# A fused attention and feed-forward layer on one core: W_o by seven quarters, sums with one PSUM operand, two roots at a time, another tail

## The chip, the cores and the metric

One NeuronCore of one Trainium2 chip runs the whole kernel. The metric is the device time of one execution in microseconds. The engines are TensorE (PE, matmuls; PEld is its weight load), VectorE (DVE), ScalarE (ACT) and GpSimd (POOL); SyncE (SP) issues most DMAs. [...] Matmuls write PSUM[...]; the rest of the working data is in SBUF.

## What is computed

Cut to what matters, with x of shape (4, 2048, 256) and everything in fp32:

```python
# attention within chunks of C = 32 tokens, decayed and causal
Q, K, V = x @ W_q.T, x @ W_k.T, x @ W_v.T
S = (Qc @ Kc.T) * mask                  # mask[i, j] = decay ** (i - j), 0 for j > i
O = S @ Vc
a = x + (sigmoid(x @ W_g.T) * O) @ W_o.T + x
h = layernorm(a)                        # over the 256 features, eps 1e-5, no scale or bias
# feed-forward with int32 weights in -127..127, scaled by 1/127
r = h + (silu(h @ w_gate.T) * (h @ w_up.T)) @ w_down.T   # 256 -> 768 -> 256
out = layernorm(r)
```

## The kernel before, in words

**Blocks.** The 8192 tokens are 16 blocks (NB) of 512 (TB), each of four groups (NG) of 128. D = 256 is two chunks of 128 features and H = 768 six. x comes in twice, token by row (`x`) and feature by row (`xT`). For Q and K the kernel has one matrix M = Wq^T Wk, so that scores are x M x^T. `attn_gate`, `attn_v` and `attn_y` are plain projections and are used for blocks 0 and 1 alone.

**Seven quarters.** From block 2 on, V, y = x M and the gate are made by `seven` (L390): a product of two 2x2 arrangements of quarters with seven products of quarters in place of eight. `token_sums` (L348, POOL) and `weight_sums` (L335) make the sums of quarters that go in. The first four products go to four PSUM banks; the other three are added later onto banks 1, 5 and 7 (`others`, the "rest" in the loop). Between them ACT copies p1, p5 and p7 to SBUF (L406), DVE makes u = p6 + p1 (L408) and POOL p57 = p5 + p7 (L410). At the end ACT evicts the first quarter (L416), DVE the second and third (L417, L418, with u), and POOL makes the fourth from p57 and u (L419). `token_major` (L374) writes tokens by row with matmuls of 128x128, `feature_major` (L359) features by row with 128x256.

**Attention.** `attn_scores` (L506) takes pairs of chunks, 64 tokens, into bank ps and masks them with DVE (L524) into sT. `attn_values` (L529) makes po = v^T sT, which DVE multiplies by the gate (L542) into goT. `attn_out` (L576) multiplies goT by W_o through `project_back` (L551; matmul L561, bank pa, 128x256), adds 2x (L582), and calls `layer_norm` (L310): DVE statistics (L295, L296), ACT square root (L304), DVE reciprocal and scaling (L315, L317), and four DVE operations (L319), one for each group. Square root and sigmoid are in different tables of ACT, so a table load stands before each change (the rows of L304, L441 and L664 that say ACT_TABLE_LOAD). h is held times 2^23 (H_UP).

**Feed-forward.** h is transposed: in the loop by `move_h` (L609), four DVE transposes in squares of 32 and 16 DMAs on SP, and `split_h` (L630), which cuts it into a high part (ACT, fp32r) and a low one (POOL, fp16). In six chunks `ffn_up` (L646) makes fg and fu (L656, one bank each), a sigmoid (ACT, L664), s = fg * s (DVE, L666), u = fu * s (DVE, L668), and u's high part (ACT, L675) and low part (POOL, L676). `ffn_down` (L678) calls `project_back` (fdn), DVE adds h (L683), and `finish` (L695) normalizes and stores.

**Order.** One loop (L734 to L779) runs b from 0 to 13: the feed-forward of block b, scores, values and out-projection of block n = b + 2, projections of block m = b + 3. They are interleaved by hand as written there. Each engine keeps its own queue; the order within a queue is made by the framework from the program and its dependences, save where an instruction is pinned with `keep_in_program_order` (`in_turn`). PSUM banks go round by eight under one tag (ps), so a tile waits for whoever last read its bank. Blocks 14 and 15 end the program by hand (from L787): the feed-forward of 14 with the transposition of h_15 by PE (L598), block 15's `ffn_up` in two halves of 256 columns, and its fdn one group at a time (L853, residual L861), with moments, root and `normalize` (L803: DVE reciprocal L806, POOL shift L815, ACT scaling L824) for each; the last group is normalized by DVE (L876, L877).

**Wide weights.** `look_up` (L258) takes the largest magnitude of the six halves of the weights (L261, one at each of the first six turns of the loop); `count_wide` (L270) compares them, sums over partitions with a small matmul (pw, L277), and gives n_wide, called just before block 15's fdn. A branch for weights beyond 127 uses n_wide after the end; these inputs don't take it.

Of the kernel before, what the change touches and what calls it, by code (L numbers as in the profile page):

```python
# [54 lines left out]
P = 128  # L55
# [10 lines left out]
U_UP = 2.0**-3  # L66
WARM = 2
# [3 lines left out]
def kernel(  # L71
# [184 lines left out]
    top = const.tile([P, 6], F32, tag="top", name="top")  # L256

    def look_up(i):  # L258
        w = (fg, fu, fd)[i // 2][0].bitcast(F32)
        half = w.shape[1] // 2  # L260
        reduced = nc.vector.tensor_reduce(  # L261
            top[:, i : i + 1],
            w[:, i % 2 * half : (i % 2 + 1) * half, :].rearrange("p k n -> p (k n)"),
            mybir.AxisListType.X,
            ALU.max,
            apply_absolute_value=True,
        )
        tc.keep_in_program_order(reduced)
# [21 lines left out]
    def moments(r, name, groups=range(NG), order=free):  # L290

        mv = small.tile([P, NG, 2], F32, tag="mv", name=f"mv_{name}")
        for g in groups:
            st = small.tile([P, 6], F32, tag="st", name=f"st_{name}_{g}")
            order(nc.vector.bn_stats(st, r[:, g, :]))  # L295
            order(nc.vector.bn_aggr(mv[:, g, :], st))  # L296
        return mv
# [12 lines left out]
    def layer_norm(dst, r, name, on_r=1.0, on_dst=1.0):  # L310


        mv = moments(r, name)
        rstd = root(mv, name, on_r)
        nc.vector.reciprocal(rstd, rstd)  # L315
        if on_dst != on_r:
            nc.vector.tensor_scalar(rstd, rstd, on_dst / on_r, None, ALU.mult)  # L317
        for g in range(NG):
            nc.vector.tensor_scalar(  # L319
                dst[:, g, :],  # L320
                r[:, g, :],
                mv[:, g, 0:1],
                rstd[:, g : g + 1],
                ALU.subtract,
                ALU.mult,
            )
# [21 lines left out]
    def token_sums(t, name):  # L348

        out = sums.tile([P, 4, HB], F32, tag="sums", name=f"{name}_sums")  # L350
        t1, t3, t2, t4 = (out[:, i, :] for i in range(4))
        b11, b12, b21, b22 = (t[:, k, n * HB : (n + 1) * HB] for k in range(2) for n in range(2))
        nc.gpsimd.tensor_tensor(t1, b12, b11, ALU.subtract)
# [5 lines left out]
    def feature_major(a, b):  # L359


        def product(i, pb, first):
            nc.tensor.matmul(  # L363
                pb,
                lhsT=a[i - 1],
                rhs=b[i - 1],
                start=first,
                stop=True,
                skip_group_check=True,
            )  # L370

        return product

    def token_major(a, b):  # L374


        def product(i, pb, first):
            for g in range(HB // P):
                nc.tensor.matmul(  # L379
                    pb[:, g * P : (g + 1) * P],  # L380
                    lhsT=b[i - 1][:, g * P : (g + 1) * P],
                    rhs=a[i - 1],
                    start=first and g == 0,
                    stop=True,
                    skip_group_check=True,
# [4 lines left out]
    def seven(name, product, quarter, func=AF.Copy):  # L390
# [9 lines left out]
        banks = {i: bank(f"p{i}_{name}")[:, :HB] for i in (1, 5, 7, 6)}  # L400
        p = {}
        for i, pb in banks.items():
            product(i, pb, True)
            if i != 6:
                p[i] = part(f"p{i}")
                nc.scalar.copy(p[i], pb)  # L406
        u = part("p6")
        nc.vector.tensor_tensor(u, banks[6], p[1], ALU.add)  # L408
        p57 = part("p57")
        nc.gpsimd.tensor_tensor(p57, p[5], p[7], ALU.add)  # L410

        def others():
            for i, onto in ((2, 1), (3, 5), (4, 7)):
                product(i, banks[onto], False)
            c11, c12, c21, c22 = (quarter(i, j) for i in range(2) for j in range(2))
            nc.scalar.activation(c11, shaped(banks[1], c11), func)  # L416
            nc.vector.tensor_tensor(c12, shaped(banks[5], c12), shaped(u, c12), ALU.add)  # L417
            nc.vector.tensor_tensor(c21, shaped(banks[7], c21), shaped(u, c21), ALU.add)  # L418
            nc.gpsimd.tensor_tensor(c22, shaped(p57, c22), shaped(u, c22), ALU.add)  # L419
# [86 lines left out]
    def attn_scores(b, yT):  # L506
# [16 lines left out]
        for rows in halves:  # L523
            nc.vector.tensor_tensor(  # L524
                sT[rows, :, rows], ps[rows], mask[rows], ALU.mult
# [3 lines left out]
    def attn_values(b, sT, v, sg):  # L529
        goT = work.tile([P, KD, TB], F32, tag="goT", name=f"goT_{b}")  # L530
        for dc in range(KD):
# [10 lines left out]
            nc.vector.tensor_tensor(goT[:, dc, :], po, sg[:, dc, :], ALU.mult)  # L542
# [33 lines left out]
    def attn_out(b, goT, up=H_UP):  # L576
# [3 lines left out]
        def residual(gs, pb):  # L580

            nc.vector.scalar_tensor_tensor(  # L582
                flat(r, gs), flat(xn, gs), 2.0, pb, ALU.mult, ALU.add
            )

        project_back(b, (chunked(goT),), (chunked(wo),), residual, "pa")
        layer_norm(r, r, f"a{b}", on_dst=up)
        return r

# [19 lines left out]
    def move_h(b, h):  # L609
# [5 lines left out]
        for g in range(NG):  # L615
            nc.vector.transpose(
                sq[:, :, g, :], h[:, g, :].rearrange("p (j f) -> p j f", f=SQ)
# [28 lines left out]
    def ffn_up(b, hT, uT, chunks, cols=slice(0, TB)):  # L646
        n = cols.stop - cols.start
        for hc in chunks:
# [16 lines left out]

            nc.vector.scalar_tensor_tensor(s, pg, U_UP / H_UP**2, s, ALU.mult, ALU.mult)  # L666
            u = work.tile([P, n], F32, tag="u", name=f"u_{b}_{hc}")
            nc.vector.tensor_tensor(u, pu, s, ALU.mult)  # L668
# [5 lines left out]
            hi, lo = uT[0][hc][:, cols], uT[1][hc][:, cols]  # L674
            nc.scalar.copy(hi, u)  # L675
            nc.gpsimd.tensor_tensor(lo, u, hi.bitcast(F32), ALU.subtract)  # L676

    def ffn_down(b, uT, h):  # L678
        r = work.tile([P, NG, D], F32, tag="r2", name=f"r2_{b}")

        def residual(gs, pb):
# [3 lines left out]
            )  # L685

        project_back(b, uT, [chunked(w) for w in fd], residual, "fdn")
        return r
# [6 lines left out]
    def finish(b, r, start=None):  # L695
        layer_norm(r, r, f"f{b}", on_r=H_UP)
# [8 lines left out]
    yT = attn_y(0)  # L705
    v_1 = attn_v(1)
    fg = integers(ffn_gT, ffn_int[0], "fg")
# [9 lines left out]
    sT_1 = attn_scores(1, yT)  # L717
    xTs[3] = load_xT(3)
# [13 lines left out]
    looked = 0  # L732

    for b in range(NB - 2):  # L734
# [6 lines left out]
        yT, v, sg = ahead  # L741
        ffn_up(b, hT, uT, range(0, 1))
# [7 lines left out]
        moving = move_h(b + 1, hs[b + 1])  # L750
# [3 lines left out]
        ffn_up(b, hT, uT, range(3, 4))  # L754
        if more:
            v_rest()
        goT = attn_values(n, sT, v, sg)
        if more:
            y_next, y_rest = split_y(m, x_sums)
        ffn_up(b, hT, uT, range(4, 5))  # L760
        if more:
            y_rest()
            hTs[b + 1] = split_h(b + 1, moving)
        ffn_up(b, hT, uT, range(5, KH))
        if more:
            sg_next, g_rest = split_gate(m, x_sums)
        hs[n] = attn_out(n, goT, 1 if n == NB - 1 else H_UP)
        if more:
            g_rest()
            ahead = y_next, v_next, sg_next  # L770
        if m + 1 < NB:
            x_sums = token_sums(xTs[m + 1], f"x_{m + 1}")
        r = ffn_down(b, uT, hs.pop(b))
        if not more:
            hTs[b + 1] = split_h(b + 1, moving)
        finish(b, r)
        if looked < top.shape[1]:
            look_up(looked)
            looked += 1  # L779
    for i in range(looked, top.shape[1]):  # L780
        look_up(i)
# [15 lines left out]
    r_before = ffn_down(last - 1, uT, hs[last - 1])  # L797
    mv_before = moments(r_before, f"f{last - 1}")
    ffn_up(last, hTs[last], uT_last, range(len(early), KH), cols[0])
    ffn_up(last, hTs[last], uT_last, range(KH), cols[1])  # L800
    n_wide = count_wide()

    def normalize(r, mv, rstd, name, on_r=1.0, groups=range(NG)):  # L803

        span = slice(groups[0], groups[-1] + 1)
        in_turn(nc.vector.reciprocal(rstd[:, span], rstd[:, span]))  # L806
        if on_r != 1:
            in_turn(
                nc.vector.tensor_scalar(
                    rstd[:, span], rstd[:, span], 1 / on_r, None, ALU.mult  # L810
                )
            )
        shift = small.tile([P, NG], F32, tag="shift", name=f"shift_{name}")
        for g in groups:
            nc.gpsimd.tensor_scalar(  # L815
                shift[:, g : g + 1],
                mv[:, g, 0:1],
                rstd[:, g : g + 1],
                -1.0,
                ALU.mult,  # L820
                ALU.mult,
            )
        for g in groups:
            scaled = nc.scalar.activation(  # L824
                r[:, g, :],
                r[:, g, :],
                AF.Identity,
                bias=shift[:, g : g + 1],
                scale=rstd[:, g : g + 1],
            )  # L830
            in_turn(scaled)

    std_before = root(mv_before, f"f{last - 1}", H_UP, order=in_turn)
    r = work.tile([P, NG, D], F32, tag="r2", name=f"r2_{last}")

    def store_group(g):
        tokens = slice(last * TB + g * P, last * TB + (g + 1) * P)
        nc.sync.dma_start(out[tokens, :], r[:, g, :])

    waiting = []

    def normalize_first():
        g, mv, std = waiting.pop(0)
        normalize(r, mv, std, f"f{last}_{g}", groups=[g])
        store_group(g)

    for g in range(NG):
# [16 lines left out]
        if g == 0:  # L866
            normalize(r_before, mv_before, std_before, f"f{last - 1}", H_UP)
            store(last - 1, r_before)
        std = root(mv, f"f{last}_{g}", groups=[g], order=in_turn)
        waiting.append((g, mv, std))  # L870
        if 0 < g < NG - 1:
            normalize_first()
        if g == NG - 2:
            normalize_first()
# [119 lines left out]
```

## Time and profile before

| | |
|---|---|
| median of three runs | 536.26 us (535.37 to 536.46) |
| the profiled execution | 535.63 us |
| its span in the profile | 533.9 us |
| what lies around the span | 1.7 us |
| one block of the loop | 32.0 us |
| PE's last matmul ends | 524.3 us into the span |
| DVE's last normalization ends | 529.0 us |

Views of the profile used here: the page (busy time of each engine, and shares of the chain of work that ended last); the waits of an engine (who it waited for, us in total, times, longest); windows (busy time of each engine in a stretch); the chain in order of time; the timeline of an engine (start and length in us, engine, line, operation, out<-in with partitions x elements, in square brackets the idle time before it and who ended it); and groups of instructions by form (busy us, mean ns of one, idle before). L numbers are lines of the kernel of that profile. A "record" is one matmul in the trace; an fp32 matmul leaves two.

### The profile page before, as it was taken

The numbers are of one execution on the slowest core, as the hardware profiler recorded it, in microseconds if no ns is written. First come the engines' busy times: TensorE is split into PE (matmuls) and PEld (weight loads), VectorE is DVE, ScalarE is ACT, GpSimd is POOL, SyncE is SP. The second block draws the span as 40 slices with busy tenths as digits, with TensorE's granted clock in tenths as the row PEclk, the third lists the DMA queues.
The fourth block names the chain that finished last, engine by engine and source line by source line (L and its number), as shares of the span: only waits on it lengthen the run. The fifth ranks groups of instructions, "written<-read, shape, count | busy, mean of one in ns | idle before, by whom it ended". The sixth has DMA issues, their size and how long they took to land.

```text
span 533.9 us, 9939 instructions
## 1 busy us (share of the span) xinstructions
PE 522.8 (98%) x3486; PEld 421.0 (79%) x3486; DVE 391.2 (73%) x1026; ACT 310.8 (58%) x561; POOL 268.4 (50%) x305
## 2 busy tenths in 40 slices
PE   8999999999999999999999999999999999999992
PEld 5688887888878788887888878788887888868792
DVE  4468659587695867859587695867859587698883
ACT  2284556555564754656555664764657566566754
POOL 5132672735636365572735636374572736433651
PEclk9999999999999999999999999999999999999997
DMA  7531312214130231412214130231412113020102
GB/s 253 181 120 39 80 40 69 52 41 119 42 101 18 52 108 41 114 46 63 58 39 120 41 105 15 54 107 40 112 49 78 42 43 78 1 65 16 40 2 82
DMA packets 43126, 36.87 MB, mean 69 GB/s; under 512 B 4673, under 2 KB 38977, under 8 KB 43073
## 3 DMA queue, kind: packets, MB, share of 16 engines
q1 hardware_dynamic: 41952, 35.15, 23.3%
q10 hardware_dynamic: 1088, 1.05, 0.6%
q8 instruction: 29, 0.48, 0.4%
q14 instruction: 25, 0.20, 0.1%
q0 software_dynamic: 32, 0.00, 0.0%
HBM read 20.45 MB, written 8.39 MB: 54 GB/s over the span
## 4 chain that ended last, share of the span: by engine, by line
PE 95%; DVE 2%; ACT 1%; issue 0%; DVEq 0%; POOL 0%
PE fg L656 16%; PE fdn L561 16%; PE fu L656 15%; PE pa L561 10%; PE p_v L379 8%; PE p_y L363 8%; PE p_g L363 8%; PE po L535 5%; PE ps L514 3%; PE pg L459 1%; PE py L475 1%; PE pv L494 1%; PE pi L177 1%; DVE u L668 1%; DVE s L666 1%
## 5 line engine op out<-in xcount | busy, mean ns | idle before, releaser
L676 POOL TENSOR_TENSOR u_lo<-u,u_hi 128x512 f16<-128x512 f32 (+1 forms) x102 | 123.7, 1214 | 144.3 <-ACT u_hi L675 143.8
L666 DVE SCALAR_TENSOR_TENSOR s<-fg,s 128x512 f32<-128x512 f32 (+1 forms) x102 | 66.4, 651 | 48.1 <-ACT s L664 47.6
L664 ACT ACTIVATE s<-fg 128x512 f32<-128x512 f32 (+1 forms) x102 | 58.2, 571 | 66.6 <-PE fg L656 65.9
L675 ACT CAST u_hi<-u 128x512 fp32r<-128x512 f32 (+1 forms) x102 | 60.4, 592 | 31.5 <-DVE u L668 30.7
L656 PE MATMUL fg<-hT_hi,fg_hi 128*128 128x512 f32 (+1 forms) x204 | 74.0, 443 | 0.0
L668 DVE TENSOR_TENSOR u<-fu,s 128x512 f32<-128x512 f32 (+1 forms) x102 | 66.1, 650 | 5.0 <-POOL u_lo L676 1.0
L656 PE MATMUL fu<-hT_hi,fu_hi 128*128 128x512 f32 (+1 forms) x204 | 61.6, 382 | 0.0
L656 PE MATMUL fg<-hT_lo,fg_lo 128*128 128x512 f16 (+1 forms) x204 | 58.9, 370 | 0.0
L656 PE MATMUL fu<-hT_lo,fu_lo 128*128 128x512 f16 (+1 forms) x204 | 58.1, 366 | 0.0
L561 PE MATMUL pa<-wo,goT 128*128 128x256 f32 x256 | 58.0, 379 | 0.0
L561 PE MATMUL fdn<-fd_hi,u_hi 128*128 128x256 f32 x360 | 55.4, 296 | 0.0
L561 PEld LDWEIGHTS pa<-wo,goT 128*128 128x128 f32 x256 | 48.6, 190 | 6.7
L640 POOL TENSOR_TENSOR hT_lo<-hT,hT_hi 128x512 f16<-128x512 f32 x28 | 35.4, 1286 | 28.5 <-ACT hT_hi L639 28.5
L561 PEld LDWEIGHTS fdn<-fd_hi,u_hi 128*128 128x128 f32 x360 | 46.8, 189 | 1.1
L561 PE MATMUL fdn<-fd_lo,u_lo 128*128 128x256 f16 x360 | 44.7, 274 | 0.0
L656 PEld LDWEIGHTS fu<-hT_hi,fu_hi 128*128 128x128 f32 x204 | 37.5, 188 | 7.7
L656 PEld LDWEIGHTS fg<-hT_hi,fg_hi 128*128 128x128 f32 x204 | 35.7, 189 | 8.5
L304 ACT ACT_TABLE_LOAD x30 | 38.5, 1283 | 0.5
L656 PEld LDWEIGHTS <-fu_lo 128*128 128x128 f16 x204 | 20.0, 98 | 21.5 <-DVE sT L524 1.2
L561 PEld LDWEIGHTS <-u_lo 128*128 128x128 f16 x360 | 32.7, 98 | 5.1 <-POOL u_lo L676 0.3
L582 DVE SCALAR_TENSOR_TENSOR h<-x,pa 128x512 f32<-128x512 f32 x32 | 22.0, 688 | 17.5 <-PE pa L561 16.9
L535 PE MATMUL po<-sT,v 128*128 128x128 f32 x256 | 31.2, 275 | 0.0
(150 smaller groups left out, 983.7 us busy)
## 6 DMA issues: line engine op xcount, KB each, us to landing
x<-in_x_dram SPq DMA_DIRECT2D x16, 512.0 KB, 3.4
xT<-in_xT_dram SPq DMA_DIRECT2D x15, 512.0 KB, 4.4
out_dram<-r SPq DMA_DIRECT2D x15, 512.0 KB, 5.1
hT<-sq SPq DMA_DIRECT2D x224, 32.0 KB, 1.9
fg_int<-in_ffn_gT_dram SPq DMA_DIRECT2D x3, 256.0 KB, 8.1
fu_int<-in_ffn_uT_dram SPq DMA_DIRECT2D x3, 256.0 KB, 6.5
fd_int<-in_ffn_dT_dram SPq DMA_DIRECT2D x3, 256.0 KB, 6.0
xT<-in_xT_dram SPq DMA_DIRECT2D x2, 256.0 KB, 3.8
```

Source lines behind the costliest of these rows:

```text
L304: nc.scalar.activation(std[:, span], mv[:, span, 1], AF.Sqrt, bias=eps, scale=1 / on_r**2)
L363: nc.tensor.matmul(pb, lhsT=a[i - 1], rhs=b[i - 1], start=first, stop=True, skip_group_check=True,)
L379: nc.tensor.matmul(pb[:, g * P : (g + 1) * P], lhsT=b[i - 1][:, g * P : (g + 1) * P], rhs=a[i - 1], start=first and g == 0, stop=True, ski ...
L535: nc.tensor.matmul(po[:, cols], lhsT=v[:, g, dc * P : (dc + 1) * P], rhs=sT[:, cols], start=True, stop=True,)
L561: nc.tensor.matmul(pb[:, j * D : (j + 1) * D], lhsT=part[:, g * P : (g + 1) * P], rhs=w, start=(i == 0), stop=(i == len(terms) - 1),)
L640: nc.gpsimd.tensor_tensor(in_order[1], whole, in_order[0].bitcast(F32), ALU.subtract)
L656: nc.tensor.matmul(pb, lhsT=w[kind][:, dc, hc * P : (hc + 1) * P], rhs=hT[kind][:, dc, cols], start=(kind == kinds[0] and dc == 0), stop=( ...
L664: nc.scalar.activation(s, pg, AF.Sigmoid, scale=SCALE / H_UP)
L666: nc.vector.scalar_tensor_tensor(s, pg, U_UP / H_UP**2, s, ALU.mult, ALU.mult)
L668: nc.vector.tensor_tensor(u, pu, s, ALU.mult)
L675: nc.scalar.copy(hi, u)
L676: nc.gpsimd.tensor_tensor(lo, u, hi.bitcast(F32), ALU.subtract)
```

## The change

1. **W_o.** W_o is halved at the start (ACT). The out-projection of blocks 2 to 14 goes by seven quarters (`split_out`), with sums of W_o's quarters made once and sums of goT's quarters for each block (POOL). x is added as it is: POOL adds it to u (twice) and to p57, DVE adds it to the first quarter. The normalization takes the halved sum into account (on_r = HALF). Blocks 0, 1 and 15 keep `project_back`, with the residual now a plain sum.
2. **Sums.** p57 is made by DVE from bank 7 and the copy of p5; ACT's copy of p7 is gone. c22 is made at once after it, not in `others`. The banks are taken in the order 1, 6, 5, 7.
3. **Norms in the loop.** DVE makes statistics and reciprocal, POOL a scale and a shift (three small operations), ACT the normalization, four operations. h is normalized at the start of the next block, ahead of its first sigmoid; r_b is normalized and stored two blocks later, after the values. Both roots stand together after `split_out`, and a one-column sigmoid after them brings the sigmoid table back. In the last turn of the loop (b = 13) r_12 and r_13 are both normalized at its end.
4. **Order.** In turns 1 to 12 the DVE operations of `seven`, scores, values and `ffn_up` are pinned (`in_steady_turn`); chunk 4 and 5 of `ffn_up` stand together ahead of y's rest; the product u_3 is held until v's rest; `move_h` is at the head of the block, `split_h` after the out-projection.
5. **Search.** `look_up` reads the nine int32 pieces as they land (128x512 each): five at the start, four in turn 0 after the values, followed by `count_wide`. Its matmul then stands between po of block 2 and p_y of block 3.
6. **Tail.** The roots stand ahead of the normalizations. r_15's groups 0 and 1 and r_14's 0 and 1 are normalized by ACT, r_14's 2 and 3 by POOL, r_15's 2 and 3 by DVE; all are stored by group, two of them from ACT's queue.

The core of the diff:

```diff
-        banks = {i: bank(f"p{i}_{name}")[:, :HB] for i in (1, 5, 7, 6)}
+        banks = {i: bank(f"p{i}_{name}")[:, :HB] for i in (1, 6, 5, 7)}
         p = {}
         for i, pb in banks.items():
             product(i, pb, True)
-            if i != 6:
+            if i in (1, 5):
                 p[i] = part(f"p{i}")
                 nc.scalar.copy(p[i], pb)
-        u = part("p6")
-        nc.vector.tensor_tensor(u, banks[6], p[1], ALU.add)
-        p57 = part("p57")
-        nc.gpsimd.tensor_tensor(p57, p[5], p[7], ALU.add)
+        u, p57 = part("p6"), part("p57")
+        in_steady_turn(nc.vector.tensor_tensor(u, banks[6], p[1], ALU.add))
+        in_steady_turn(nc.vector.tensor_tensor(p57, banks[7], p[5], ALU.add))
+        c11, c12, c21, c22 = (quarter(i, j) for i in range(2) for j in range(2))
+        to_c12 = to_c21 = u
+        if plus is not None:
+            x11, x12, x21, x22 = (plus(i, j) for i in range(2) for j in range(2))
+            to_c12, to_c21 = part("to_c12"), part("to_c21")
+            for t, xq in ((to_c12, x12), (to_c21, x21)):
+                nc.gpsimd.tensor_tensor(shaped(t, xq), shaped(u, xq), xq, ALU.add)
+            nc.gpsimd.tensor_tensor(shaped(p57, x22), shaped(p57, x22), x22, ALU.add)
+        nc.gpsimd.tensor_tensor(c22, shaped(p57, c22), shaped(u, c22), ALU.add)
...
+    def scale_and_shift(mv, std, kind, name):
...
+        in_turn(nc.vector.reciprocal(std, std))
+        for t, sign in ((minus, -1.0), (scale, 1.0)):
+            nc.gpsimd.tensor_scalar(t, std, sign * on_dst / on_r, None, ALU.mult)
+        nc.gpsimd.tensor_tensor(shift, mv[:, :, 0], minus, ALU.mult)
+        return scale, shift
+
+    def normalize(r, scale, shift):
+        for g in range(NG):
+            in_turn(
+                nc.scalar.activation(
+                    r[:, g, :],
+                    r[:, g, :],
+                    AF.Identity,
+                    bias=shift[:, g : g + 1],
+                    scale=scale[:, g : g + 1],
+                )
+            )
...
+    def split_out(b, goT_sums):
+
+        xn = xns.pop(b)
+        r = norm.tile([P, NG, D], F32, tag="h", name=f"h_{b}")
+        product = token_major(w_sums["o"], goT_sums)
+        others = seven(f"o_{b}", product, by_tokens(r), plus=by_tokens(xn))
+
+        def rest():
+            others()
+            return moments(r, f"a{b}")
+
+        return r, rest
...
     for b in range(NB - 2):
...
+        if b:
+            normalize(hs[b + 1], *scales_h)
+        moving = move_h(b + 1, hs[b + 1])
         ffn_up(b, hT, uT, range(0, 1))
...
-        ffn_up(b, hT, uT, range(3, 4))
+        multiply = ffn_up(b, hT, uT, range(3, 4), held=True)
         if more:
             v_rest()
+        multiply()
         goT = attn_values(n, sT, v, sg)
+        if scales_out is not None:
+            normalize(r_before, *scales_out)
+            store(b - 2, r_before)
+        if b == 0:
+            look_up(range(5, n_pieces))
+            n_wide = count_wide()
         if more:
+            go_sums = token_sums(goT, f"go_{n}")
             y_next, y_rest = split_y(m, x_sums)
-        ffn_up(b, hT, uT, range(4, 5))
+        ffn_up(b, hT, uT, range(4, KH))
+        r_before = r_out
         if more:
             y_rest()
+            sg_next, g_rest = split_gate(m, x_sums)
+            hs[n], out_rest = split_out(n, go_sums)
+            g_rest()
+            mv_h = out_rest()
...
             hTs[b + 1] = split_h(b + 1, moving)
-        ffn_up(b, hT, uT, range(5, KH))
-        if more:
-            sg_next, g_rest = split_gate(m, x_sums)
-        hs[n] = attn_out(n, goT, 1 if n == NB - 1 else H_UP)
...
+            std_h = root_in_turn(mv_h, of_h, f"h_{b}")
+            if b:
+                mv_before, std_before = mv_out, root_in_turn(mv_out, of_out, f"out_{b}")
+
+            in_turn(nc.scalar.activation(table, eps, AF.Sigmoid))
...
+        else:
+            hs[n] = attn_out(n, goT, 1)
             hTs[b + 1] = split_h(b + 1, moving)
+            mv_before, std_before = mv_out, root_in_turn(mv_out, of_out, f"out_{b}")
+            r_out, mv_out, _ = ffn_down(b, uT, hs.pop(b))
+            std = root_in_turn(mv_out, of_out, f"last_{b}")
+            for block, r, mv, of_r in (
+                (b - 1, r_before, mv_before, std_before),
+                (b, r_out, mv_out, std),
+            ):
+                normalize(r, *scale_and_shift(mv, of_r, of_out, f"f{block}"))
+                store(block, r)
...
         if g == 0:
-            normalize(r_before, mv_before, std_before, f"f{last - 1}", H_UP)
-            store(last - 1, r_before)
-        std = root(mv, f"f{last}_{g}", groups=[g], order=in_turn)
...
+            std_before = root(mv_before, f"f{before}", H_UP, order=in_turn)
+        of_group.append((mv, root(mv, f"f{last}_{g}", groups=[g], order=in_turn)))
...
+            for g_before in (2, 3):
+                by_vector(nc.gpsimd, r_before, g_before, mv_before, std_before)
+            by_scalar(r_before, 0, std_before, shift_before[:, 0:1])
...
+    for g in (2, 3):
+        mv, std = of_group[g]
+        inverse(std, slice(g, g + 1))
+        by_vector(nc.vector, r, g, mv, std)
+        store_group(last, r, g)
+    for g in (1, 3):
+        store_group(last - 1, r_before, g, nc.scalar)
```

## The prediction

> **What bounds the kernel now.** I read first the page's busy times and chain of work, then TensorE's waits, then one steady block, then the places that the diff touches.
>
> ```profile
> PE 522.8 (98%) x3486; PEld 421.0 (79%) x3486; DVE 391.2 (73%) x1026; ACT 310.8 (58%) x561; POOL 268.4 (50%) x305
> PE 95%; DVE 2%; ACT 1%; issue 0%; DVEq 0%; POOL 0%
> ```
>
> ```profile
> PE pi L177 <- DVE idle L174: 1.5, 1, 1.5
> ```
>
> ```profile
> 109.74:141.75 32.01, 32.01 (x219) 26.08 (x218) 24.46 (x63) 19.26 (x34) 17.17 (x18) 1.00 0.25 67
> ```
>
> TensorE (PE) makes 95% of the chain and waits once, 1.5 us at the start. The window of one block of the loop (length; then PE, weight loads, DVE, ACT, POOL) shows PE busy for all 32.01 us at full clock, DVE for 24.46, ACT 19.26, POOL 17.17. So work taken from the other engines is worth nothing as long as PE stays fed; only fewer PE microseconds, or the 9.6 us after PE's last matmul (524.3 to 533.9), can gain, and each new PE wait costs its full length.
>
> [...] The trace of before shows no matmul passing another, so a matmul placed early in the order holds all behind it; two steps below rest on this. [...] The trace has the 1.283 us, but the square root follows 0.01 us behind the load (492.11 + 1.28, 493.40), so I use 1.28. [...]
>
> **1. W_o by seven quarters.** In the chain, one block's out-projection and V projection (start, us, what):
>
> ```profile
> 265.03 3.45 PE pa L561 x16
> ...
> 281.98 1.78 PE p_v L379 x16
> ...
> 285.54 1.34 PE p_v L379 x12
> ```
>
> pa is 16 records of 128x256. The new product has exactly p_v's form: 28 records of 128x128, 1.78 + 1.34 = 3.12 us. Saved: 3.45 - 3.12 = 0.33 a block, not the eighth that the count of products suggests (0.43), since a short record costs 0.111 us and a long one 0.216. Blocks 2 to 14 use it, 13 in all: **-4.3 us** (-4.0 to -4.6 by where the pieces are cut).
>
> **2. The other engines in a steady block.** DVE loses eight normalizations (0.41 each) and the residual's 2 x 0.69, and gains four p57 sums, u and three quarter sums of o (8 x 0.42), and loses the 0.95 reduce: near 22.3 busy. ACT loses two table loads (2 x 1.28) and three copies (3 x 0.37), gains two copies (0.37) and eight normalizations (2 x 2.07, at the tail's rate below): 20.4. POOL gains four sums of goT, three additions of x and one c22, less three p57 (in all 5 x 0.73), and the small scale and shift operations (6 x 0.265): 22.4. All stay under 31.7, so what counts is order. I followed the built order with 0 at the block's first fg matmul (115.3 in the block above). hT_lo leaves POOL at -2.3; three x sums (0.7 each) and three small operations give the shift at +0.8; four ACT normalizations end at +2.9, and only then does the first sigmoid run, where it could at +1.4 before. Its product leaves DVE at +4.2; its bank is asked for at +7.2. Followed alike: u_1 ready +6.2, wanted +8.5; masked scores +7.0, +9.0; p57 of v +9.2, +11.2; the held product u_3 +12.7, +15.6; hT_lo -2.3, +1.0. The nearest is p57 of the out-projection with 1.7 to spare. Cost **0**; the cover is 1.7 to 3 us of slack, and if a row is later than its slack, the excess is paid 13 times. Moved DMAs: the sixteen issues of hT on SP, which wait for DVE's transposes, now stand ahead of xT's load; xT lands 4.4 us after its issue and POOL wants it near the block's end, over 15 us later, so nothing waits.
>
> **3. The search for wide weights.** Five of nine reduces stand in the start-up while PE works on projections: 0. Four, with the count, stand in block 0 behind the second goT, and the count's small matmul stands between po and p_y in PE's order.
>
> ```profile
> 62.85 1.79 PE po L535 x16
> 64.64 1.73 PE p_y L363 x8
> ```
>
> ```profile
> 64.67 0.69 DVE L542 TENSOR_TENSOR goT<-po,sg 128x512 f32<-128x512 f32 x1 [0.18 <-PE po L535]
> ```
>
> ```profile
> L261 DVE TENSOR_REDUCE top<-fg_hi 128x1 f32<-128x768 f32 x2 | 1.9, 946 | 0.0
> ```
>
> po ends at 64.64 and goT at 65.36. An estimate for a reduce of 512 elements from the 946 ns of 768: 946 x 512/768 = 0.63 us. Four end at 67.7 or so, the comparison (a 128x9 operation, 0.2) near 68.0. PE, ready for p_y at 64.64, stands until then: **+3.4 us** (2.7 if the reduces overlap as far as neighbouring DVE rows, 3.9 if each has 0.75). Queued behind on PE is everything else. Not paid back: DVE and ACT catch up, but PE has no slack. The six 0.95 us reduces that leave the loop freed DVE time that nothing waited for: 0.
>
> **4. The end of block 13.** There r_12 and r_13 are normalized by eight ACT operations, placed ahead of u_hi_0 and the second sigmoid of block 14. ACT before:
>
> ```profile
> 491.49 0.60 ACT L664 ACTIVATE s<-fg 128x512 f32<-128x512 f32 x1 [2.43 <-PE fg L656]
> 492.11 1.28 ACT L304 ACT_TABLE_LOAD   x1
> 493.40 0.30 ACT L304 ACTIVATE rstd_f<-mv_f,eps 128x4 f32<-128x4 f32 x1
> 493.72 1.28 ACT L664 ACT_TABLE_LOAD   x1
> 495.01 0.60 ACT L664 ACTIVATE s<-fg 128x512 f32<-128x512 f32 x1
> ```
>
> ```profile
> 523.03 2.07 ACT L824 ACTIVATE r<-r,shift_f,rstd_f 128x256 f32<-128x256 f32 x4 [0.82 <-POOL shift_f L815]
> ```
>
> Four normalizations take 2.07 in the tail (second fence), so eight take 4.1: from 493.7 to 497.8. u_hi_0 (0.5) and the load (1.28) put the sigmoid at 499.7, its end at 500.2, and DVE's product with fg (0.69) at 500.9. The fifth chunk's fg needs that bank; PE wants it here:
>
> ```profile
> 498.16 0.46 PE fg L656 x2
> ```
>
> So PE stands 2.75 us. Behind that, ACT and DVE hold three chunks of backlog: the sixth chunk's first product ends at 507.45 where fdn_14, shifted, would start at 507.05 (+0.4), and u_lo_5, behind three 1.28 us subtractions on POOL, at 510.2 where it is wanted at 509.6 (+0.6). Sum **+3.75**, taken as +4.0 for hand-offs that I didn't count (low 2.7, only the first wait; high 4.7).
>
> **5. The tail.**
>
> ```profile
> 525.32 0.16 DVE L806 RECIPROCAL rstd_f<-rstd_f 128x1 f32<-128x1 f32 x1 [1.69 <-ACT rstd_f L304]
> ...
> 528.58 0.41 DVE L877 TENSOR_SCALAR r<-r,mv_f,rstd_f 128x256 f32<-128x256 f32 x1
> ```
>
> DVE waits 1.69 us for a root that stands behind four ACT normalizations, while PE's last product is there at 524.3. After, roots come first: last residual 524.3 to 524.7, moments to 525.3, root 525.6, reciprocal and two DVE normalizations to 526.45, against 528.99. **-2.5 us** (-1.5 to -3.1: the two POOL normalizations, not in this trace, could end last; POOL's rows of this size take 0.73, and at twice that they end near 526.5). The 4.9 us from there to the end of the span, the last store, stays.
>
> **6. The rest.** Halving W_o (0.6 on ACT, behind v's copies), the sums of W_o (five POOL rows, 2.3 us) and blocks 0 and 1 hide beside PE's start-up work; if o_sums delays block 2's x sums, up to +0.5.
>
> **Sum.** -4.3 + 3.4 + 4.0 - 2.5 = +0.6. The profiled run took 535.63 (span 533.9), so 536.2; it lies 0.63 under the median 536.26, against which I forecast **536.9**. By the ends of the terms, -2.0 to +3.3: 534.3 to 539.6. A measurement tells about 0.2% (1.07 us) from no change.
>
> **Rivals.** (a) Faster: the two single waits are shorter. If the eight normalizations run at an ACT copy's 0.372 us for this size, they end at 496.7, the first wait is 1.65 and the backlog behind it gone; with the count and the tail at their low ends, -4.3 + 2.7 + 1.7 - 3.1 = -3.0: 533.3. For: only seven rows of the tail stand behind the 0.52. Against: a copy has no scale and bias to read, and the order is fixed. 0.22. (b) Slower: one steady hand-off fails, at the head of the block. The normalizations stand ahead of the sigmoid, on data that passes DVE, ACT and POOL; POOL runs at 22.4 of 31.7. If the shift is over 3 us later than I have it (from 3.8 after the first fg on), PE waits for the first chunk's bank in each of 13 blocks; 0.3 us of excess is 3.9, so 540.8. For: POOL's durations are rough, and its queue is new. Against: 3 us of room. 0.28. (c) The quarters save nothing, as their weight loads (192 ns) show where the streams (111 ns apart) are short: +4.3, 541.2. Against: p_v has that very form at full rate. 0.03, counted with (b)'s side. The sum as worked out: 0.47.
>
> **How the numbers follow.** Of the 0.47, 0.35 lies within 0.2%, 0.09 above, 0.03 below. So faster 0.03 + 0.22 = 0.25, same 0.35, slower 0.09 + 0.31 = 0.40. The range takes in most of (a) and about half of (b) and (c): 532.5 to 541.0; it leaves out two in ten. The likeliest case's own range is 534.3 to 539.6.
>
> **What would show it.** PE's waits get two new rows: the count's matmul for DVE, 3 to 3.5 us, once; block 14's fg for DVE, 2.7 or more, once, and fdn for POOL behind it. Out-projection pieces sum to 3.12; a steady block is 31.7 long with PE busy throughout; the last DVE normalization is 2.2 us after PE's last matmul. I am wrong if PE waits in every block, if either row is missing, or if the block is still 32.0.

## The result, and the profile after

| | before | after |
|---|---|---|
| median (lowest to highest), four runs each | 535.99 us (535.37 to 536.46) | 540.05 us (539.32 to 540.62) |
| ratio, 95% interval | | 1.0075 (1.0062 to 1.0088) |
| profiled execution, its span | 535.63, 533.9 us | 540.2, 538.4 us |

The change costs 4.1 us, 0.75%. The forecast was 536.9, some 3 us too low: its range (532.5 to 541.0) held the time, but the case that it worked out (534.3 to 539.6) did not. First the page of after: busy times, shares of the chain of work, and the granted TensorE clock in 40 slices.

```profile
PE 521.3 (97%) x3642; PEld 423.1 (79%) x3642; DVE 388.9 (72%) x979; ACT 320.3 (59%) x638; POOL 330.4 (61%) x450
PEclk9999979999999999999999999999999999999898
PE 95%; DVE 2%; ACT 2%; issue 0%
```

PE is still 95% of the chain. New in the clock's line, apart from the end of the program, are a 7 among the nines, in the slice from 67.3 to 80.8 us, and an 8 in the one from 498.0 to 511.5. PE's busy time fell by only 1.5 us where seven quarters in 13 blocks should take 4.3 away: some of its work ran slower. PE's waits (us in total, times, longest):

```profile
PE pw L279 <- DVE wide L275: 3.6, 1, 3.6
PE fg L733 <- DVE s L743: 2.8, 1, 2.8
PE pi L178 <- DVE idle L175: 1.5, 1, 1.5
```

Both forecast rows are there, once each: 3.6 us where 3 to 3.5 was forecast, 2.8 where 2.7 or more was. The row that the prediction put behind the second, fdn for POOL, is missing. No wait repeats block by block. The windows of after (length; PE, weight loads, DVE, ACT, POOL busy; granted clock; DMA):

```profile
66.00:68.00 2.00, 0.33 (x3) 0.31 (x4) 1.58 (x4) 0.00 (x0) 1.42 (x3) 0.60 0.54 203
68.00:70.00 2.00, 2.00 (x5) 1.63 (x6) 0.22 (x3) 0.37 (x1) 0.00 (x0) 0.50 0.00 0
...
141.43:173.02 31.59, 31.59 (x230) 26.09 (x229) 23.49 (x58) 19.95 (x41) 21.80 (x29) 1.00 0.22 67
...
504.00:506.00 2.00, 2.00 (x6) 0.98 (x5) 2.00 (x4) 0.96 (x2) 2.00 (x2) 0.50 0.00 0
```

A steady block is 31.59 us long with PE busy throughout at full clock. But behind each of the two waits PE stands "busy" at a clock of 0.50. Finer windows put the fall at 66.4 and the return at 73.2 (6.8 us), then 503.3 and 506.7 (3.4 us). The first fall comes 1.3 us before its wait ends, the second 1.7 us after. The chain of after (start, us, what) shows what that costs:

```profile
62.26 1.80 PE po L599 x16
...
64.08 0.69 DVE goT L606
64.78 2.38 DVE top L263 x4
...
67.18 0.36 DVE wide L275
...
67.67 0.20 PE pw L279 x2
67.88 3.71 PE p_y L409 x8
71.58 0.85 PE fg L733 x2
72.44 0.85 PE fu L733 x2
73.29 0.48 PE fg L733 x2
```

p_y takes 3.71 us where before it took 1.73 for the same eight records; fg and fu take 0.85 each, and 0.48 or less once the clock is back. That is 2.8 us on top of the wait, and half of the 5.6 us (67.67 to 73.2) that PE works at half clock. Where the time went, by pieces of both chains:

| stretch | after less before, us | of it |
|---|---|---|
| start-up, to the end of po in block 0 | -0.6 | the execution's, see below |
| block 0, from there to its fdn | +6.3 | wait 3.6, count's matmul 0.2, half clock 2.8; quarters -0.3 |
| fdn of block 0 to fdn of block 13 | -5.0 | twelve blocks of 31.59, not 32.00 |
| start of fdn of block 13 to the end of fdn of block 14 | +4.5 | wait 2.8; the rest is taken up in number 6 |
| from there to PE's last matmul | -0.3 | the count's matmul, 0.2, is gone |
| PE's last matmul to DVE's last normalization | -2.3 | 4.7 to 2.4 |
| DVE's last normalization to the end of the span | +1.9 | 4.9 to 6.8 |
| sum | +4.5 | spans: 538.4 - 533.9 |

The first row isn't the change's. The first projection of before, of after, and of number 10 below, which starts as after does:

```profile
5.24 3.99 PE pg L459 x8
...
5.17 3.46 PE pg L523 x8
...
5.24 3.99 PE pg L527 x8
```

The same eight records take 3.99, 3.46 and 3.99 us, and po of block 0 ends at 64.64, 64.06 and 64.64. So this 0.6 us comes and goes between executions of one start-up.

### The profile page after: what moved, and what is told of

It reads as the page before. It is cut to its first block, busy times and chain, and to the rows that moved or that the text cites. A ratio compares the mean times of both kernels' runs of the same rounds, so it can differ in the third digit from the quotient of the medians.

```text
span 538.4 us, 10518 instructions
## 1 busy us (share of the span) xinstructions
PE 521.3 (97%) x3642; PEld 423.1 (79%) x3642; DVE 388.9 (72%) x979; ACT 320.3 (59%) x638; POOL 330.4 (61%) x450
## 4 chain that ended last, share of the span: by engine, by line
PE 95%; DVE 2%; ACT 2%; issue 0%
PE fg L733 16%; PE fu L733 16%; PE fdn L625 15%; PE p_y L409 8%; PE p_v L427 8%; PE p_g L409 8%; PE p_o L427 8%; PE po L599 5%; PE ps L578 3%; PE pa L625 2%; PE py L539 1%; PE pv L558 1%; PE pg L523 1%; PE pi L178 1%; ACT r L364 1%; PE fdn L977 1%
## 5 line engine op out<-in xcount | busy, mean ns | idle before, releaser
L741 ACT ACTIVATE s<-fg 128x512 f32<-128x512 f32 (+1 forms) x102 | 56.7, 569 | 40.2 <-PE fg L733 40.0
L733 PE MATMUL fg<-hT_hi,fg_hi 128*128 128x512 f32 (+1 forms) x204 | 75.7, 453 | 2.8 <-DVE s L743 2.8
L625 PE MATMUL fdn<-fd_hi,u_hi 128*128 128x256 f32 x360 | 52.9, 289 | 0.0
L625 PEld LDWEIGHTS fdn<-fd_hi,u_hi 128*128 128x128 f32 x360 | 45.1, 189 | 0.4
L364 ACT ACTIVATE h<-h,shift_h,scale_h 128x256 f32<-128x256 f32 x52 | 27.0, 592 | 22.6 <-POOL shift_h L358 22.6
L733 PEld LDWEIGHTS <-fu_lo 128*128 128x128 f16 x204 | 20.0, 98 | 21.8 <-issue 0.6
L772 DVE SCALAR_TENSOR_TENSOR r<-fdn,h 128x512 f32<-128x512 f32 x30 | 20.7, 691 | 20.4 <-PE fdn L625 20.4
L733 PEld LDWEIGHTS <-fg_lo 128*128 128x128 f16 x204 | 16.0, 99 | 20.7 <-issue 13.2
L599 PEld LDWEIGHTS po<-sT,v 128*128 128x128 f32 x256 | 30.0, 192 | 0.6 <-issue 0.5
```

What stands on the lines that cost most here:

```text
L364: nc.scalar.activation(r[:, g, :], r[:, g, :], AF.Identity, bias=shift[:, g : g + 1], scale=scale[:, g : g + 1],)
L599: nc.tensor.matmul(po[:, cols], lhsT=v[:, g, dc * P : (dc + 1) * P], rhs=sT[:, cols], start=True, stop=True,)
L625: nc.tensor.matmul(pb[:, j * D : (j + 1) * D], lhsT=part[:, g * P : (g + 1) * P], rhs=w, start=(i == 0), stop=(i == len(terms) - 1),)
L733: nc.tensor.matmul(pb, lhsT=w[kind][:, dc, hc * P : (hc + 1) * P], rhs=hT[kind][:, dc, cols], start=(kind == kinds[0] and dc == 0), stop=( ...
L741: nc.scalar.activation(s, pg, AF.Sigmoid, scale=SCALE / H_UP)
```

## The experiments

**Theory A:** each of PE's two waits is paid for twice, by its length and then by TensorE at half clock behind it, and nothing else makes the change slower. **Theory B:** the waits cost their length alone; the clock falls for another reason and would stay. Numbers 1 to 4 ran on one chip (before there: 535.82), 5, 6, 7 and 9 together on another (535.84), 8, 10 and 11 together (535.46).

**1. The count behind y's rest.** DVE's comparison stays where it is; only the small matmul, and what reads it, moves.

```diff
-            n_wide = count_wide()
+            found = find_wide()
...
             y_rest()
+            if b == 0:
+                n_wide = count_wide(*found)
```

> The count's matmul is moved from between the values and y of block 0 to behind y's rest; the reduces stay. Theory A (a wait of TensorE costs its length and then a stretch at half clock): the 3.63 us wait, the small matmul's 0.2 and the 2.8 us that the matmuls behind it took longer all go, about 6.6 less than the changed kernel's 540.05, so 533.4. Theory B (as predicted: the wait costs only its length, and the slow matmuls behind it have another cause, such as operands that come late): 3.8 less, 536.2.

534.23 us (533.27 to 535.16), ratio 0.9969 (0.996 to 0.9977). One matmul of 0.2 us, moved, gives 5.8 us, 1.6 times the wait that it removes. PE's waits and a window of this kernel:

```profile
PE fg L737 <- DVE s L747: 2.7, 1, 2.7
PE pi L178 <- DVE idle L175: 1.5, 1, 1.5
```

```profile
498.00:500.00 2.00, 2.00 (x7) 0.89 (x5) 2.00 (x5) 0.99 (x2) 2.00 (x2) 0.50 0.00 0
```

The first wait and the 7 in the clock's line are gone; the second wait and its 0.50 stay. The time is nearer to A's 533.4 than to B's 536.2, and from po's end to fdn of block 0 the profile is 6.3 us shorter than after's. A holds for block 0.

**2. The same wait, with PE kept busy.** Four idle products, into the bank that the count then overwrites, ahead of the count's matmul, change no result and leave the wait's end where DVE sets it.

```diff
         pw = bank("pw")
+        for _ in range(4):
+            nc.tensor.matmul(pw, lhsT=idle[:, :P], rhs=idle, start=True, stop=True)
```

> Four idle matmuls of 128x512 (about 3.45 us at full clock) are put ahead of the count's matmul, into its own bank, so that TensorE works through the wait; the wait for VectorE itself stays. Theory A: granted clock stays 1.0 in this place, the y matmuls take 1.73 again in place of 3.71, 2.8 less than the changed kernel: 537.2. Theory B: nothing changes, 540.0.

537.41 us (536.95 to 537.88), ratio 1.0027 (1.0015 to 1.0038). The timeline of PE in this kernel, and one window:

```profile
64.82 3.60 PE L280 MATMUL pw<-idle 128*128 128x512 f32 x8
68.53 0.20 PE L281 MATMUL pw<-wide,ones 128*1 128x9 f32 x2
```

```profile
68.00:70.00 2.00, 1.89 (x9) 1.30 (x9) 0.84 (x5) 0.37 (x1) 0.45 (x1) 1.00 0.00 0
```

The count's matmul is as far behind po as in after, the clock stays at 1.00, and 2.6 us come back, which is the half-clock part by itself (2.8 in the chain). B expected none of it. So in this wait it is PE's idleness that takes the clock, and this loss comes on top of the wait's length.

**3 and 4. The end of block 13, one way.** r_12 is normalized on ACT before fdn of block 13, and r_13 on DVE, in after (3) and with the count behind y's rest as well (4).

```diff
             mv_before, std_before = mv_out, root_in_turn(mv_out, of_out, f"out_{b}")
+            normalize(r_before, *scale_and_shift(mv_before, std_before, of_out, f"f{b - 1}"))
+            store(b - 1, r_before)
             r_out, mv_out, _ = ffn_down(b, uT, hs.pop(b))
...
-                normalize(r, *scale_and_shift(mv, of_r, of_out, f"f{block}"))
+                in_turn(
+                    nc.vector.tensor_scalar(
+                        r_out[:, g, :], r_out[:, g, :], mv_out[:, g, 0:1],
+                        std[:, g : g + 1], ALU.subtract, ALU.mult,
+                    )
+                )
```

> At the end of block 13, r_12 is normalized by ScalarE ahead of fdn_13's end, where ScalarE was idle, and r_13 by VectorE; no normalization stands ahead of block 14's second sigmoid. Theory A: the 2.8 us wait of fg of block 14 and about 2.0 us of half clock behind it go, 4.8 less than the changed kernel: 535.3. Theory B (the wait, and a backlog of ScalarE and VectorE behind it, 4.0 in all): 536.0. If VectorE's normalizations now hold up the first chunk, less than 4 is gained.

> Both moves together (the count later, the end of block 13 eased). Theory A: 11.4 less than the changed kernel, 528.6, and TensorE waits nowhere but in the first microseconds. Theory B: 7.8 less, 532.2. In both it is faster than the kernel before (535.99).

Number 3: 537.3 us (534.5 to 538.84), ratio 1.0026 (1.0017 to 1.0035): 2.8 gained, less than either theory had. Number 4: 531.61 us (531.01 to 532.03), ratio 0.9923 (0.9906 to 0.9939): between the two, nearer to B's 532.2. PE's waits in 4, and the ACT row that makes them:

```profile
PE fg L737 <- DVE s L747: 0.5, 1, 0.5
PE fdn L629 <- POOL u_lo L762: 0.4, 1, 0.4
PE fdn L629 <- ACT u_hi L761: 0.3, 1, 0.3
```

```profile
486.87 2.08 ACT L368 ACTIVATE r<-r,shift_f,scale_f 128x256 f32<-128x256 f32 x4 [3.77 <-POOL shift_f L362]
```

I had made a new wait: ACT stands 3.77 us for POOL's shift, with the next sigmoid behind it, and 1.2 us of that reach PE. So neither kernel tells A from B in block 14. The spread of number 3, 4.3 us, is larger than that of 4 (1.0), which lacks block 0's wait. It goes with the clock: of its 20 runs the two fastest (534.5 and 535.1) have a mean granted clock of 0.995 and 0.994, as those of number 4 have (0.995 to 0.996), and the 16 slowest 0.989 to 0.992. A fall of 6.8 us takes 0.006 off the mean (half of 6.8 in the span of 537.1), so in those two the clock didn't fall so in block 0; 6 has such a case.

**5. Whole products with W_o.** `split_out` is replaced in the loop by `project_back`, as before; all else is after's.

```diff
-            hs[n], out_rest = split_out(n, go_sums)
+            hs[n], out_rest = whole_out(n, goT)
```

> The out-projection of blocks 2 to 14 goes back to whole products (16 records of 128x256, bank pa), the rest of the changed kernel stays. If the quarters are what shortens a block: a block takes 32.0 again and the run 12 x 0.41 + 0.33 = 5.3 more than the changed kernel's 540.05, so 545.3. If the 0.08 of a block that the prediction didn't have (fdn 5.51 before, 5.43 after) comes from the order of the steps and not from the quarters: 12 x 0.33 + 0.33 = 4.3 more, 544.3. If the quarters save nothing: 540.

544.54 us (542.48 to 545.05), ratio 1.017 (1.0153 to 1.0187): 4.5 over after, near the 4.3 of the second expectation. The total is blurred, since in the profiled run, the fastest of the four, the clock didn't fall in block 0 and fell for longer in block 14 (see 6); a steady block is not. The chains of after and of this kernel:

```profile
241.40 5.43 PE fdn L625 x48
...
268.57 1.78 PE p_o L427 x16
...
271.65 1.34 PE p_o L427 x12
272.99 5.43 PE fdn L625 x48
```

```profile
208.85 5.43 PE fdn L625 x48
...
236.02 3.45 PE pa L625 x16
...
240.77 5.43 PE fdn L625 x48
```

From fdn to fdn after takes 31.59 and this kernel 31.92, before 32.00. So the quarters are worth 0.33 a block (3.45 - 1.78 - 1.34), and the new order another 0.08: fdn takes 5.43 us in both, 5.51 before.

**6. Two of the four reduces ahead of v's quarters.** This was to shorten the first wait.

```diff
+        if b == 0:
+            look_up(range(5, 7))
         if more:
             v_next, v_rest = split_v(m, x_sums)
...
-            look_up(range(5, n_pieces))
+            look_up(range(7, n_pieces))
```

> Two of the four reduces ahead of the count are moved to an earlier place in block 0 where VectorE is idle, so the wait of TensorE is about 2.4 us in place of 3.63. If the loss is in proportion to the wait: 6.6 x 2.4/3.63 = 4.4, 2.2 less than the changed kernel, 537.8. If half clock comes in whole stretches of 3.4 us (6.8 were seen behind the 3.63 us wait, 3.4 behind the 2.8 us wait): one stretch in place of two, 1.2 + 1.1 to 1.4 less, 537.6 or so, with PE's clock at 0.5 for 3.4 us. If a wait of 2.4 is too short for the clock to drop: 1.2 + 2.8 less, 536.0.

539.48 us (538.11 to 539.79), ratio 1.0064 (1.0044 to 1.0084): all expectations missed, 0.6 gained. The wait shrank by 0.8 only, since the comparison now took 0.73 us, against 0.36, and the clock still fell for 6.8 us: a wait shorter by a fifth brought the same fall. The run gave something else. Here block 14's wait brought no fall of the clock. Waits of this kernel, and a window:

```profile
PE fg L733 <- DVE s L743: 2.7, 1, 2.7
...
PE fdn L625 <- ACT u_hi L757: 0.7, 1, 0.7
PE fdn L625 <- POOL u_lo L758: 0.4, 1, 0.4
```

```profile
502.00:504.00 2.00, 2.00 (x10) 0.99 (x10) 2.00 (x4) 1.52 (x4) 0.74 (x1) 1.00 0.00 0
```

With PE at full clock the backlog that the prediction's step 4 named appears: 0.7 + 0.4, worked out there as 0.4 + 0.6. In after PE was so slow behind the wait that the others caught up. Yet the stretch is no shorter here. fdn of block 13 and the end of fdn of block 14, in the chains of before, of after and of this kernel:

```profile
484.57 5.52 PE fdn L561 x48
...
506.56 3.82 PE fdn L561 x32
```

```profile
485.32 5.48 PE fdn L625 x48
...
510.04 5.54 PE fdn L625 x48
```

```profile
485.08 5.48 PE fdn L625 x48
...
509.59 1.29 POOL u_lo L758
...
510.92 4.36 PE fdn L625 x37
```

From the start of the one to the end of the other they take 25.8, 30.3 and 30.2 us; number 1, where the clock fell too, takes 30.25. In after as here, POOL's u_lo, for which fdn waits here, ends 25.8 us behind the start. So in block 14 A fails: a fall of 3.4 us cost nothing on top of the wait and the backlog, 4.5 us in all. The three waits listed above make 3.8 of it here; the rest was not traced. Of number 1's 13 runs, too, the four with the highest mean clock (0.996) are not the faster ones (534.52 to 535.16). Only in number 5, where the fall in block 14 lasted 6.8 us, is the stretch longer, 31.6 us, of which 0.3 is a longer wait.

Why no fall? The traces don't settle it. Their slow stretches last 3.4 us (block 14 of after and of number 1) or 6.8 (block 0 of after and of this kernel, block 14 of number 5). In the 3.4 us ahead of a fall PE was idle for 2.35 us in block 0 of after (63.0 to 66.4), for 1.76 in its block 14 (499.9 to 503.3) and for 2.0 in number 1. But this kernel's wait in block 14 is 2.7 us of idle PE, and nothing falls. Number 5 has the plainest case, in block 0: a wait nearly as long as after's, the clock at 1.00 behind it, and p_y in 1.92 us, not 3.71.

```profile
PE pw L279 <- DVE wide L275: 3.5, 1, 3.5
```

```profile
68.00:70.00 2.00, 2.00 (x10) 1.75 (x10) 0.73 (x4) 0.75 (x2) 0.00 (x0) 1.00 0.00 0
```

```profile
67.87 1.92 PE p_y L409 x8
```

So of two waits of 3.5 and 3.6 us one lost 2.8 us to the clock and the other nothing, and a wait of 2.8 us brought a fall in after's block 14. The length of a wait doesn't decide it alone; what else does was not shown.

**7 and 8. The end of block 13, without the new wait.** The count stands behind y's rest; r_12 is normalized by POOL and r_13 by DVE, behind the first chunk of block 14. Number 8 is the same kernel again on another chip.

```diff
-                normalize(r, *scale_and_shift(mv, of_r, of_out, f"f{block}"))
+            for eng, block, r, mv, of_r in (
+                (nc.gpsimd, b - 1, r_before, mv_before, std_before),
+                (nc.vector, b, r_out, mv_out, std),
+            ):
...
+                    eng.tensor_scalar(
+                        r[:, g, :], r[:, g, :], mv[:, g, 0:1],
+                        of_r[:, g : g + 1], ALU.subtract, ALU.mult,
+                    )
```

> Count later as in e1; at the end of block 13 r_12 is normalized by GpSimd, idle there, and r_13 by VectorE behind the first chunk's products, as in the kernel before. Theory A: no wait of TensorE in block 14 and no drop of its clock: e1's 534.23 less 4.8, 529.4. If VectorE's or GpSimd's normalizations hold up a chunk by as much as in e4 (waits of 0.5, 0.4 and 0.3), it is no better than e4's 531.6.

> The same kernel as e7, on the chip of e10 and e11, to compare with: 529.75.

529.75 us (529.62 to 530.62), ratio 0.989 (0.9874 to 0.9907); again 529.67 (529.24 to 530.22), ratio 0.9886 (0.9869 to 0.9904). PE's waits in 7:

```profile
PE pi L178 <- DVE idle L175: 1.5, 1, 1.5
PE fdn L629 <- POOL u_lo L762: 0.4, 1, 0.4
```

Both waits are gone and no window from 488 to 504 has a clock under 1.00. From number 1 to 7 the end of block 13 gives 4.5 us, where A had 4.8 and B 4.0, so this doesn't tell them apart. This version beats before by 1.1% and after by 1.9%.

**9. The old tail.** Number 4 with before's tail.

```diff
-        of_group.append((mv, root(mv, f"f{last}_{g}", groups=[g], order=in_turn)))
...
+        if g == 0:
+            normalize_old(r_before, mv_before, std_before, f"f{last - 1}", H_UP)
+            store(last - 1, r_before)
+        std = root(mv, f"f{last}_{g}", groups=[g], order=in_turn)
```

> e4 with the tail of the kernel before (roots behind the normalizations, r_14 by ScalarE and stored whole, r_15 by group). As predicted (the new tail is worth 2.5): 531.6 + 2.5 = 534.1. By the two traces (the last normalization 2.3 earlier, but the stores behind it 1.9 longer, since r_14's half megabyte now moves at the same time as r_15's): 0.4 more, 532.0.

532.65 us (532.28 to 533.2), ratio 0.9943, against number 4's 531.61: 1.0 us, though the two ran on different chips and their intervals of the ratio overlap. The profiles say the same. From PE's last matmul to DVE's last normalization the old tail takes 4.8 us and the new one 2.4, but from there to the end 5.3 and 6.5.

**10 and 11. Is it the stores?** In the new tail the groups' stores stand close together. Theory: they land late because they move at once. Number 10 is 7 with half of r_14 rooted, normalized and stored earlier; number 11 is 7 without r_14's four stores (rows of block 14 of the output aren't written). The edit shown is number 11's.

```diff
-            for g_before in (0, 2):
-                store_group(last - 1, r_before, g_before)
...
-    for g in (1, 3):
-        store_group(last - 1, r_before, g, nc.scalar)
```

> e7 with the first half of r_14 taken out of the tail: its root is taken by ScalarE in the gap behind block 14's first fdn bank, GpSimd normalizes the two groups there, and both are stored then, 256 KB some 9 us ahead of the end. If the stores at the end are held up by the bytes that move together (1.05 MB in about 3 us at 344 GB/s, stores ending 1.35 us later behind the last normalization than in the kernel before): about 1.0 less than e7's 529.75, 528.8. If the issue of the last stores or their fixed cost is what counts: 529.7. If the early root holds up block 15's sigmoids: above 530.

> e7 without the four stores of r_14, so that block 14's rows of the output are left unwritten; all else is computed. If r_14's half megabyte, moving together with r_15's, is what makes the end of the span 6.25 us behind the last normalization (4.9 in the kernel before, where it had been stored earlier): about 1.3 less than e7's 529.75, 528.4. If it isn't, 529.7.

530.04 us (529.68 to 530.56), ratio 0.9897 (0.9879 to 0.9915), and 529.19 us (528.53 to 530.66), ratio 0.9885 (0.9865 to 0.9904): no gain, and at most 0.5. From the last normalization to the end: 5.9 and 5.7 us, where number 8 has 6.1 and before 4.9. Up to the landing of the last store it is 3.3 and 3.2, 4.0 in number 8 and 2.9 in before; from there to the end 1.9 to 2.6 in all four. But the nine profiles with one and the same new tail take 6.1 to 7.0 from the last normalization to the end, so half a microsecond between two of them tells little. The theory explains a part at most; what holds the rest, some 0.8 us, stays open.

## Why the prediction was right or wrong

**Step 1, the quarters: right.** 0.33 a block, from records of the same form, measured as 0.33. The loop gave 5.3 and not 4.3, because fdn became 0.08 shorter a block in the new order, which no step looked at.

**Step 2, the steady block: right.** No wait repeats. DVE 23.5 against 22.3, ACT 19.95 against 20.4, POOL 21.8 against 22.4; block 31.59 against 31.7. Rivals (b) and (c) are excluded, (b) by the missing rows, (c) by number 5.

**Steps 3 and 4: the waits right, the cost of the first wrong.** "PE, ready for p_y at 64.64, stands until then: +3.4 us": it stood 3.6. "So PE stands 2.75 us": it stood 2.8. Both rest on matmuls keeping their order, and so it was: p_y's eight records stood behind the count's matmul through its wait of 3.6 us. ACT's eight normalizations and the sigmoid behind them, in after:

```profile
494.41 4.05 ACT L364 ACTIVATE r<-r,shift_f,scale_f 128x256 f32<-128x256 f32 x8
498.37 0.60 ACT L757 CAST u_hi<-u 128x512 fp32r<-128x512 f32 x1
498.99 1.28 ACT L741 ACT_TABLE_LOAD   x1
500.28 1.08 ACT L741 ACTIVATE s<-fg 128x512 f32<-128x512 f32 x2
```

4.05 against 4.1, which ends rival (a). The failed term is step 3's +3.4, priced by an assumption of the first part, "each new PE wait costs its full length". In block 0 an idle PE also lost its clock: 2.8 (number 2 gives back 2.6 with the wait kept), besides 0.2 of a longer wait and 0.2 for the count's own matmul, so 6.6 against 3.4. The loss isn't there in every execution: behind number 5's first wait, of 3.5 us, the clock stayed at 1.00. In block 14 the clock fell too, but the wait and the backlog behind it, step 4's own mechanism, are what was paid: 4.5 against 4.0. The profile of before could not show the clock's part, as its PE never stood for over 1.5 us.

**Step 5, the tail: half right.** "the last DVE normalization is 2.2 us after PE's last matmul": 2.4. But "The 4.9 us from there to the end of the span, the last store, stays" failed: 6.8. In the two profiles the tail gains 0.4 in place of 2.5; the timed pair of 4 and 9 says 1.0. From PE's last matmul to the end the nine profiles with the new tail take 8.4 to 9.3 us, the two with the old one 9.6 and 10.1.

**Step 6 and the sum.** The start-up of the profiled run was 0.6 shorter by chance, and PE's last stretch 0.3; neither was worked out. Forecast +0.6; the misses are -1.0 (loop), +3.2 (block 0), +0.5 (block 14), +2.1 (tail) and -0.9 (these two), together +3.9, so +4.5, as the spans differ; the medians differ by 4.1. The ends of the terms add up to -2.3 and +3.1 (+3.6 with step 6), not to -2.0 and +3.3; the measured time lies above them either way.

**Luck.** That the range held the time is luck. Its upper end was there for rivals (b) and (c), on which most of the 0.40 for slower rested too, and neither came true; and the loss from the clock was in part made up by the shorter fdn, which no step had either.

## What to carry to other kernels

A wait of a busy TensorE is priced at its length and at what follows it, here half clock for the matmuls behind it (0.50 for 3.4 or 6.8 us) or a backlog of the other engines: a wait of 3.6 us cost 6.4 with a fall of the clock, one of 3.5 about its length without one, and one of 2.8 with a backlog 4.5 in both cases. After a wait, look at the granted clock, since PE shows as busy there (2.00 of 2.00 us at 0.50 in after). A small matmul that depends on another engine (a count, a sum over partitions) belongs behind matmuls that are ready (5.8 us in number 1), and if a wait can't be moved, idle matmuls in it can keep the clock, as in number 2 (1.00 in place of 0.50, 2.6 us). In a tail, follow the last store to the end of the program: work that ends earlier on an engine isn't yet a shorter span (the last normalization 2.3 us nearer to PE's last matmul, the end 1.9 us farther behind it).

## What the runs showed of the hardware that I had not expected

- The length of a wait alone doesn't tell whether the clock falls: the wait of 2.7 to 2.8 us brought 3.4 us at 0.50 in after and number 1, none in number 6; one of 3.6 us brought 6.8 in after, one of 3.5 us none in number 5.
- A fall of the clock need not cost time: in block 14 fdn ends as late at full clock, where it waits for POOL (30.2 us from the start of fdn of block 13, number 6), as with 3.4 us at half clock (30.3, after).
- The clock can stay at half while PE works: it was 0.50 for 6.8 us in block 0 of after and of number 6, though PE was idle for only 1.26 and 0.6 us of that, at its beginning. Where the fall came after the wait's end, with PE busy throughout (block 14 of after and of number 1), it lasted 3.4.
- One start-up isn't always equally long: its first projection took 3.46 us in after, and 3.99 in before and number 10.
